# The first pass of a two-layer image kernel: groups of 1, 4, 4, ... tiles, and three of them by Strassen's seven block products

## The chip, the cores and the metric

The kernel runs on one core of one Trainium2 chip. The metric is the device time of the kernel in microseconds (us); three runs of the kernel before have a median of 2600.22 us (2597.3 to 2600.9). The engines are TensorE (PE; its weight loads are PEld), VectorE (DVE), ScalarE (ACT), GpSimd (POOL) and SyncE (SP, which issues most DMAs). Each engine runs its own instructions in the order in which the program lists them.

## The reference, cut to what matters

The input x has 2 images of 56 x 56 pixels with 384 channels, so 6272 tokens, 49 tiles of 128. All is float32. Layer 0 is a neighbourhood attention and then an MLP. Layer 1 is a projection to 768 channels, a 3x3 depthwise convolution with four decaying scans over the image, a projection back, and an MLP.

```python
# layer 0, after the attention
y = layer_norm(x, ln2_g, ln2_b)
x = x + gelu(y @ w1 + b1) @ w2 + b2          # 384 -> 1536 -> 384
# layer 1
h = _layernorm(x, n1_g, n1_b)
p = h @ w_in + b_in                          # 384 -> 768
local = depthwise_conv3x3(p, k_conv)
mixed = 0.25 * (lr + rl + tb + bt) + local   # decaying scans of local, four directions
x = x + (layernorm(mixed) @ w_out + b_out)   # 768 -> 384
h2 = _layernorm(x, n2_g, n2_b)
return x + gelu(h2 @ w1 + b1) @ w2 + b2
```

## The kernel before, in words

The program has three stages: the attention of layer 0 (not touched, ends near 666 us), a first pass over the tokens (`passes`, from L1446), and a second pass (from L1799) whose second half is called the tail here.

**First pass.** It walks over `groups`, tiles in groups of 2, 3, 4, 4, ... (`sizes`, L625). For group g it does
- the first matmul of layer 0's MLP (`hidden`, L1186, by `columns`, L1176): 12 blocks of 128 hidden channels, each 3 matmuls over the 384 channels, with the group's tokens as the moving side (up to 512 wide), then a gelu on ACT,
- `project_in` (L1468) of the group before, which is called `waiting`: 6 blocks with w_in, evicted by ACT and stored to p_d,
- the second matmul (`tokens`, L1194): 12 matmuls of 384 columns for each tile; VectorE adds the residual x and measures the result x2 for the next layer norm.

Each float32 matmul is two instructions in the trace, each with a weight load of its own.

Between the 12 blocks m of the first matmul stand, written out by hand, the steps for two other groups. For the waiting group: `norm_w.shift` at m = 1 (VectorE), the normalization by ACT (`apply_by_scalar`, L239) from m = 2, `turned` (L1160, 16 transposes of 32x32 blocks by VectorE for a tile) from m = 3, `scaled` (L1169, ACT) at the last block, `store_x2` (L1492). For the next group: its statistics at m = 3 (`norm_of`), `shift` at m = 5, the normalization from m = 7, and `add_row` (L1113) at the end. The next group's `turned` and `scaled` follow behind project_in. `Norm.close` (L219) ends a set of statistics with one small VectorE operation and a pow on GpSimd; `shift` on VectorE waits for that pow. Two x tiles and two xn tiles exist at a time (pool x), so the load of group g + 2 (`load_group`, L1578, at the end of group g) can start when the last read of group g's x is over.

While the convolution has nothing to do (groups 1 to 3), tiles are turned by VectorE (`by_vector`, L1507); later the transposes are made by TensorE (`channels`, L1155). The convolution (`Band`, `Columns`, all on VectorE with some ACT and GpSimd) is dealt out by `Beside` (L115): every call of `beside.go(worth)` adds 0.9 x worth of credit and issues the next steps of the convolution while there is credit, each at a cost that the program states; `until` (L168) issues all that is left of a job. The first band's jobs exist when `project_in` has covered the first 20 lines of the image, at the end of `project_in` for group 2, which runs in group 3.

`prepare_w_out` (L1120) runs in group 1: 12 small matmul instructions, a trip through DRAM, and a pass of VectorE over w_out.

PSUM in this pass: two banks for the second matmul (y and y_end), three for transposes (ps_t) and three for the first matmul (ps_m).

**The tail.** Six groups of four tiles of the second pass do both MLP matmuls by Strassen's scheme with seven block products. `hidden_by_seven` (L1637) splits the 512 tokens into halves a and b, the first 256 of the 384 channels into two blocks of 128, and the hidden channels into halves; the third block of channels is done plainly. In each of three rounds u it issues 11 adds of 2 matmuls with 256 columns (22 instead of the plain 24 halves) into the banks ua (one), uz (two) and ub (two, reused in place: ACT copies a bank out between products). `finish(u)` completes a round in the middle of the next one; the last is called from the projection that follows. `measuring` is a generator whose steps are issued twice a round. `tokens_by_seven` (L1719) does the same for the second matmul with 192 columns. The sums that the scheme needs are made by GpSimd: `sums_of_w1` (5 operations) and `sums_of_w2` (4) once, `sums_of_input` (4) for each group, `sums_of_hidden` (3) for each round.

Of the kernel before, what the change touches and what calls it, by code (L numbers as in the profile page):

```python
# [175 lines left out]
def block_kernel(ctx: ExitStack, tc: tile.TileContext, ins: dict, out: bass.AP):  # L176
# [70 lines left out]
    def to_channels(psum, xs, dst, nch, g, b):  # L247

        n = xs[0].shape[0]
        for c in range(nch):  # L250
            tp = psum.tile([P, len(xs) * n], F32, name="tp", tag="pt")
            for k, x in enumerate(xs):
                nc.tensor.transpose(
                    tp[:, k * n : (k + 1) * n], x[:, c * P : (c + 1) * P], ident[:n, :n]
                )
            nc.scalar.activation(  # L256
                dst[:, c, : len(xs) * n], tp, AF.Identity, bias=col(b, c), scale=col(g, c)
            )
# [366 lines left out]
    sizes = [2, 3] + [NT] * ((T2 // P - 5) // NT)  # L625
# [444 lines left out]
    def passes(xs, xn, w1, w2, between=lambda ps: None):  # L1070
# [5 lines left out]
        cctx, bctx = ExitStack(), ExitStack()  # L1076
        cp = cctx.enter_context(tc.tile_pool(name="conv", bufs=2))
        ps_y = bctx.enter_context(tc.tile_pool(name="psy", bufs=1, space=PSUM))
        ps_t = bctx.enter_context(tc.tile_pool(name="pst", bufs=3, space=PSUM))
        ps_m = bctx.enter_context(tc.tile_pool(name="psm", bufs=3, space=PSUM))  # L1080
# [39 lines left out]
        def prepare_w_out():  # L1120
# [16 lines left out]
            t = flat(half("sums", "work"))  # L1137
# [17 lines left out]
        def channels(xn, n, g, b):  # L1155
            hT = io.tile([P, NC, MT], F32, name="hT")
            to_channels(ps_t, [xn[:, k, :] for k in range(n)], hT, NC, g, b)
# [18 lines left out]
        def columns(w, m, hT, n, name="mm"):  # L1176

            ps = ps_m.tile([P, MT], F32, name=name)
# [7 lines left out]
        def hidden(w1, m, hT, n, b1, name="mm"):  # L1186
            ps = columns(w1, m, hT, n, name)
# [258 lines left out]
        x = xs.pop(0)  # L1446
        hT = channels(xn, groups[0][1], "L0_conv_ln2_g", "L0_conv_ln2_b")
# [4 lines left out]
        add_row(x, groups[0][1], "b2_0")  # L1452
# [12 lines left out]
        waiting = None  # L1465
        bands = [(b, lo, hi) for b in range(B) for lo, hi in BANDS[b]]

        def project_in(g, hT, between=lambda: None):  # L1468
            t0, n = groups[g]
            pt = io.tile([P, NI, MT], F32, name="mx")  # L1470
            for m in range(NI):
# [5 lines left out]
                if m == 1:  # L1477
                    between()
# [23 lines left out]
        ln2, n1 = ("L0_conv_ln2_g", "L0_conv_ln2_b"), ("L1_conv_n1_g", "L1_conv_n1_b")  # L1502

        for g, (t0, n) in enumerate(groups):
            hid = []

            by_vector = 0 < g < last and not beside.busy()  # L1507
            preparing = prepare_w_out() if g == 1 else iter(())
            if g == last:
                beside.until((0, NI - 1))  # L1510
                load_row(0, "b2_1")
                ahead = load_mix(0)
            for m in range(NHID):
                next(preparing, None)
                if waiting is not None:
                    gw, x2w, norm_w = waiting
                    if m == 1:
                        norm_w.shift(groups[gw][1])
                    if m == 2:
                        xn_w = xp.tile([P, NT, C], F32, name="xn")  # L1520
                    if 2 <= m < 2 + groups[gw][1]:
                        norm_w.apply_by_scalar(m - 2, x2w, xn_w)
                    if by_vector and m == 2:
                        hT_w = io.tile([P, NC, MT], F32, name="hT")
                    if by_vector and 3 <= m < 3 + groups[gw][1]:
                        turned(xn_w, m - 3, hT_w)
                    if m == (11 if g == 1 else 6):
                        store_x2(gw, x2w)
                    if m == NHID - 1 and by_vector:
                        scaled(hT_w, groups[gw][1], *n1)  # L1530
                    elif m == NHID - 1:
                        hT_w = channels(xn_w, groups[gw][1], *n1)
                hid.append(hidden(w1, m, hT, n, "L0_conv_b1"))
                if g < last:
                    if m == 3:
                        x_next, n_next = xs.pop(g + 1), groups[g + 1][1]
                        norm_next = norm_of(x_next, n_next, sm)
                        norm_next.close(n_next)
                    if m == 5:
                        norm_next.shift(n_next)  # L1540
                    if m == 7:
                        xn_next = xp.tile([P, NT, C], F32, name="xn")
                    if 7 <= m < 7 + n_next:
                        norm_next.apply_by_scalar(m - 7, x_next, xn_next)
                    if m == NHID - 1:
                        add_row(x_next, n_next, "b2_0")
                if g == last:
                    measure_beside(m, 0, ahead)
                beside.go(MLP)
            for _ in preparing:  # L1550
                pass
            if g == 0:
                between(bank())
            if waiting is not None:
                project_in(gw, hT_w)
            if g == last:
                w1, w2_1, w_parts = weights(1)
                for part in w_parts[:3]:
# [412 lines left out]
```

## Time and profile before

| what | value |
|---|---|
| median of three runs | 2600.22 us |
| the profiled execution's own time | 2597.61 us |
| its span | 2595.7 us |
| TensorE busy, mean granted clock | 2575.3 us (99%), 0.999 |
| VectorE / ACT / GpSimd busy | 2004.2 / 959.2 / 406.1 us |
| first transposes and first matmul of the first pass | 666.27 and 667.34 us |
| start of group 1 / 2 / 3 / 4 on TensorE | 699.76 / 759.85 / 833.32 / 910.63 us |
| start of the tail's first round | 2157.18 us |

Times in a row of the timeline are the start in us from the start of the span, the length in us, then engine, line, operation, names (out<-in), shape and count; in brackets stand the idle time ahead of it and what ended it. The line of a helper stands for all its callers. TensorE's matmuls overlap at their ends, so that the pace of a row is read from start to start. "Busy" on GpSimd is rough.

### The profile page before, as it was taken

How to read it: one execution, taken by the hardware profiler on the slowest of the kernel's cores; microseconds unless marked ns; L12 is line 12 of the kernel's file. 1: busy time of each engine (PE TensorE's matmuls, PEld its weight loads, DVE VectorE, ACT ScalarE, POOL GpSimd, SP SyncE). 2: the span in 40 equal slices, each digit the busy share in tenths (PEclk: the TensorE clock that was granted, in tenths of full speed). 3: DMA queues.
4: the chain of work that ended last, by engine and by line, in shares of the span. 5: the costliest groups of instructions: out<-in, count | busy, mean ns of one | idle time of the engine just before them, and what ended most of it. 6: DMA issues, size and time to landing. Idle time of an engine off the chain costs nothing. (4 is left out here: it accounts for less than half of the span.)

```text
span 2595.7 us, 39312 instructions
## 1 busy us (share of the span) xinstructions
PE 2575.3 (99%) x15781; PEld 1593.0 (61%) x15782; DVE 2004.2 (77%) x3669; ACT 959.2 (37%) x1679; POOL 406.1 (16%) x404
## 2 busy tenths in 40 slices
PE   9999999999999999999999999999999999999999
PEld 5666666666555544555545555555555557888888
DVE  3888978887364687788998789889988836888871
ACT  4655655655332232322344422312233312333222
POOL 0111211111110100000010000000010042344342
PEclk9999999999999999999999999999999999999999
DMA  7422454225311132332346534433354321111000
GB/s 224 149 93 95 159 185 148 82 96 199 110 37 40 55 126 84 116 108 100 127 163 236 190 129 165 174 124 122 113 210 167 140 100 43 50 49 49 22 13 18
DMA packets 131649, 299.12 MB, mean 115 GB/s; under 512 B 10390, under 2 KB 86528, under 8 KB 129152
## 3 DMA queue, kind: packets, MB, share of 16 engines
q1 hardware_dynamic: 126512, 269.76, 30.1%
q10 hardware_dynamic: 4944, 26.74, 3.0%
q8 instruction: 126, 2.06, 0.3%
q14 instruction: 67, 0.55, 0.1%
HBM read 180.86 MB, written 115.61 MB: 114 GB/s over the span
## 5 line engine op out<-in xcount | busy, mean ns | idle before, releaser
L1180 PE MATMUL mm<-hT,w 128*128 128x512 f32 (+2 forms) x1368 | 575.0, 576 | 0.4 <-ACT hT L256 0.2
L1180 PEld LDWEIGHTS mm<-hT,w 128*128 128x128 f32 x1368 | 256.4, 190 | 286.3 <-issue 266.6
L1276 DVE SCALAR_TENSOR_TENSOR loc<-pt,taps,loc 128x990 f32<-128x990 f32 (+9 forms) x336 | 377.0, 1122 | 10.0 <-ACT loc L1258 1.7
L1191 ACT ACTIVATE hid<-mm,chan 128x512 f32<-128x512 f32 (+2 forms) x228 | 152.3, 668 | 502.0 <-PE mm L1180 502.0
L224 POOL TENSOR_TENSOR rs<-rs,mhalf 128x4 f32<-128x4 f32 (+4 forms) x72 | 89.2, 1239 | 1360.9 <-DVE rs L221 1359.9
L1198 PE MATMUL y_end<-w,hid 128*128 128x384 f32 x912 | 300.4, 486 | 0.0
L1198 PE MATMUL y<-w,hid 128*128 128x384 f32 x864 | 284.5, 486 | 0.0
L545 DVE TENSOR_TENSOR pts<-sc,bias 119x448 f32<-119x448 f32 (+5 forms) x396 | 219.0, 615 | 45.9 <-PE sc L534 45.5
L555 ACT ACTIVATE pts<-pts 119x448 f32<-119x448 f32 (+5 forms) x396 | 210.7, 573 | 107.1 <-DVE pts L545 102.5
L1198 PEld LDWEIGHTS y_end<-w,hid 128*128 128x128 f32 x912 | 172.8, 190 | 118.7
L1198 PEld LDWEIGHTS y<-w,hid 128*128 128x128 f32 x864 | 163.5, 190 | 112.5 <-issue 1.0
L1164 DVE STREAM_TRANSPOSE hT<-xn 32x96 f32<-32x96 f32 x672 | 181.2, 270 | 36.9 <-ACT xn L242 16.4
L388 PE MATMUL ps<-hT,wqkv 128*128 128x448 f32 x504 | 206.6, 554 | 2.1 <-ACT vs L433 1.5
L1180 PE MATMUL mm<-hT,w_in 128*128 128x512 f32 (+2 forms) x468 | 191.9, 569 | 0.6 <-ACT hT L256 0.6
L1180 PEld LDWEIGHTS mm<-hT,w_in 128*128 128x128 f32 x468 | 88.5, 190 | 102.0 <-issue 90.3
L388 PEld LDWEIGHTS ps<-hT,wqkv 128*128 128x128 f32 x504 | 92.0, 191 | 85.3 <-issue 75.3
L242 ACT ACTIVATE xn<-xc,sh,rs 128x384 f32<-128x384 f32 x98 | 64.7, 698 | 169.9 <-DVE sh L235 169.7
L1409 DVE STREAM_TRANSPOSE turned<-mx 32x192 f32<-32x192 f32 x336 | 123.9, 369 | 4.4
L534 PEld LDWEIGHTS sc<-qT,kT 32*100 32x100 f32 (+3 forms) x3168 | 87.8, 169 | 46.6 <-DVE sum L564 7.6
L574 PE MATMUL o<-pts,vt 100*32 100x112 f32 (+3 forms) x3168 | 115.2, 262 | 0.4 <-ACT pts L555 0.4
L534 PE MATMUL sc<-qT,kT 32*100 32x112 f32 (+3 forms) x3168 | 106.5, 269 | 3.4 <-DVE pts L545 3.4
L604 PE MATMUL ps<-wproj,og 128*128 128x384 f32 x294 | 104.8, 496 | 2.8 <-DVE og L517 2.2
(168 smaller groups left out, 3656.6 us busy)
## 6 DMA issues: line engine op xcount, KB each, us to landing
loc<-loc_d SPq DMA_DIRECT2D x24, 784.0 KB
mixed<-mix_d SPq DMA_DIRECT2D x24, 784.0 KB
mix_d<-mixed SPq DMA_DIRECT2D x24, 784.0 KB
xa<-x_d SPq DMA_DIRECT2D x23, 768.0 KB
bias<-in_bias_t ACTq DMA_DIRECT2D x13, 1344.0 KB
mx<-mix_d SPq DMA_DIRECT2D x11, 1536.0 KB
p_d<-mx SPq DMA_DIRECT2D x10, 1536.0 KB
pt<-p_d SPq DMA_DIRECT2D x18, 560.0 KB
```

Of the source, the lines that this page charges most:

```text
L388: nc.tensor.matmul(ps, lhsT=wqkv[:, c, m * P : (m + 1) * P], rhs=hT[:, c, half_of(n)], start=c == 0, stop=c == NC - 1,)
L534: nc.tensor.matmul(sc[i // 2][: w.keys, i % 2, q : q + TT], lhsT=kT[d, hg, w.keys_at + r * w.kc : w.keys_at + (r + w.rows) * w.kc], rhs=qT ...
L545: nc.vector.tensor_tensor(self.pts[:n, h : h + 2, lo:hi, :], sc[half][:n, :, at * TT : (at + hi - lo) * TT].rearrange("p h (c q) -> p h c ...
L555: nc.scalar.activation(t, t, AF.Exp)
L574: nc.tensor.matmul(o[i * HD : (i + 1) * HD, self.slot, :TT], lhsT=w.vt[:n, c, h * HD : (h + 1) * HD], rhs=self.pts[:n, i, c, :], start=c = ...
L604: nc.tensor.matmul(ps, lhsT=ogs[t // 7][:, c, at : at + P], rhs=wproj[:, c, :], start=c == 0, stop=c == NC - 1,)
L1164: nc.vector.transpose(hT[j : j + HD, :, k * P + i : k * P + i + HD], xn[i : i + HD, k, :].rearrange("p (c q) -> p c q", c=NC)[:, :, j : j ...
L1180: nc.tensor.matmul(ps[:, : n * P], lhsT=w[:, c, m * P : (m + 1) * P], rhs=hT[:, c, : n * P], start=c == 0, stop=c == NC - 1,)
L1191: nc.scalar.activation(t[:, : n * P], ps[:, : n * P], AF.Gelu, bias=col(b1, m))
L1198: nc.tensor.matmul(ps, lhsT=t[:, k * P : (k + 1) * P], rhs=w[:, m, :], start=m == 0, stop=m == len(lhs) - 1,)
L1276: nc.vector.scalar_tensor_tensor(to, pt[:, lo + dy - self.top : hi + dy - self.top, xt : xt + n], self.tap(dy, dx), to, ALU.mult, ALU.add,)
L1409: nc.vector.transpose(t[j : j + HD].rearrange("p (m c) -> p m c", m=NI)[:, :, i : i + HD], mx[i : i + HD, :, k * P + j : k * P + j + HD],)
```

## The change

The groups become 1, 4, 4, ...: one tile, then twelve groups of four. Groups 1 to 3 (`EARLY`) do both MLP matmuls with the functions of the tail, which take the bias, the source and the destination as arguments now and give back control between products. Their buffers (sums of the weights, of the input and of the hidden values) come from a pool named first, which lies where the convolution's buffers come later: it is closed at group 4, and only then are the convolution's pool and the former PSUM pools opened. Up to then the PSUM banks are those of the tail; project_in, the plain first matmul of group 0 and the first transposes use the two uz banks. `open_banks` opens these banks and clears three of them with zero matmuls. `prepare_w_out` moves from group 1 to group 4 and takes its buffer from another tag. In groups 0 to 3 the next group's statistics move from m = 3 to m = 0 and 1; in groups 1 to 3 the waiting group's tiles are turned at every other m, the next group's between the products of the second matmul, and `finish` of the last round comes behind the first column of project_in.

```diff
-    sizes = [2, 3] + [NT] * ((T2 // P - 5) // NT)
+    sizes = [1] + [NT] * (T2 // P // NT)
+    EARLY = range(1, 4)
...
-        cp = cctx.enter_context(tc.tile_pool(name="conv", bufs=2))
-        ps_y = bctx.enter_context(tc.tile_pool(name="psy", bufs=1, space=PSUM))
-        ps_t = bctx.enter_context(tc.tile_pool(name="pst", bufs=3, space=PSUM))
-        ps_m = bctx.enter_context(tc.tile_pool(name="psm", bufs=3, space=PSUM))
+        tp = fctx.enter_context(tc.tile_pool(name="first", bufs=1, reuse_waits="tile"))
...
-            t = flat(half("sums", "work"))
+            t = flat(half("sums", "out", 3))
...
-        x = xs.pop(0)
-        hT = channels(xn, groups[0][1], "L0_conv_ln2_g", "L0_conv_ln2_b")
         load_row(0, "b2_0")
...
-        def project_in(g, hT, between=lambda: None):
+        def project_in(g, hT, between=lambda: None, at=1):
...
+        def open_banks(stack, name):
+            ps_y = stack.enter_context(tc.tile_pool(name=f"psy_{name}", bufs=1, space=PSUM))
+            ps_d = stack.enter_context(tc.tile_pool(name=f"psd_{name}", bufs=1, space=PSUM))
+            ps_u = stack.enter_context(tc.tile_pool(name=f"psu_{name}", bufs=2, space=PSUM))
+            bank_b = ps_d.tile([P, 2, C // 2], F32, name="yb")
+            banks_b = [ps_d.tile([P, 2, MT // 2], F32, name=f"ub{i}") for i in range(2)]
+            zeros = tp.tile([P, MT], mybir.dt.bfloat16, name="zeros")
+            nc.vector.memset(zeros, 0.0)
+            for t in (bank_b, *banks_b):
+                t = flat(t)
+                nc.tensor.matmul(
+                    t, lhsT=zeros[:, :P], rhs=zeros[:, : t.shape[1]], start=True, stop=True
+                )
+            return ps_y, ps_u, bank_b, banks_b
+
+        ps_y, ps_u, bank_b, banks_b = open_banks(fctx, "first")
+        ps_t = ps_m = ps_u
+        tag = "uz"
+        w1_sums = sums_of_w1(w1, tp.tile([P, NC, HID // 2], F32, name="w1_t"))
+        x = xs.pop(0)
+        hT = channels(xn, groups[0][1], "L0_conv_ln2_g", "L0_conv_ln2_b")
+        add_row(x, groups[0][1], "b2_0")
+
+        for g, (t0, n) in enumerate(groups):
+            if g == EARLY.stop:
+                fctx.close()
+                cp = cctx.enter_context(tc.tile_pool(name="conv", bufs=2, reuse_waits="tile"))
+                ps_y = bctx.enter_context(tc.tile_pool(name="psy", bufs=1, space=PSUM))
+                ps_t = bctx.enter_context(tc.tile_pool(name="pst", bufs=3, space=PSUM))
+                ps_m = bctx.enter_context(tc.tile_pool(name="psm", bufs=3, space=PSUM))
+                tag = "pt"
+            early = g in EARLY
+            by_vector = early or 0 < g < last and not beside.busy()
+            preparing = prepare_w_out() if g == EARLY.stop else iter(())
...
+            def ahead_of(m):
...
+                    if m == 1:
+                        norm_w.shift(nw)
+                    if m == 2:
+                        xn_w = xp.tile([P, NT, C], F32, name="xn")
+                    if 2 <= m < 2 + nw:
+                        norm_w.apply_by_scalar(m - 2, x2w, xn_w)
...
+                    k = (m - 3) // 2 if early else m - 3
+                    if by_vector and 0 <= k < nw and (m % 2 == 1 or not early):
+                        turned(xn_w, k, hT_w)
+                    if m == 6:
+                        store_x2(gw, x2w)
+                    if m == NHID - 1 and by_vector:
+                        scaled(hT_w, nw, *n1)
...
+            def behind(m):
...
+                    if g < EARLY.stop and 2 * m < n_next:
+                        for k in range(2 * m, min(2 * m + 2, n_next)):
+                            norm_next.add(k, [x_next[:, k, :]])
...
+                    if m == (1 if g < EARLY.stop else 3):
+                        norm_next.close(n_next)
+                    if m == 5:
+                        norm_next.shift(n_next)
...
+                    if 7 <= m < 7 + n_next:
+                        norm_next.apply_by_scalar(m - 7, x_next, xn_next)
+                    if m == NHID - 1:
+                        add_row(x_next, n_next, "b2_0")
+
+            def both():
+                for m in range(NHID):
+                    ahead_of(m)
+                    behind(m)
+                    if m % 2 == 1:
+                        yield
+
+            if early:
+                s1, s2 = (tp.tile([P, NHID // 2, MT // 2], F32, name=x) for x in ("s1", "s2"))
+                low, high, finish = hidden_by_seven(
+                    hT, xsums, w1, w1_sums, (s1, s2), both(), "L0_conv_b1"
+                )
+                project_in(waiting[0], hT_w, finish, 0)
...
+            if early:
+                for i, _ in enumerate(tokens_by_seven(low, high, s1, s2, w2, w2_sums, x, x2)):
+                    if 0 <= i < n_next:
+                        turned(xn_next, i, hT)
+                    if i == 5:
+                        scaled(hT, n_next, *ln2)
+                        xsums = sums_of_input(hT) if g + 1 in EARLY else None
+                    if i == 6:
+                        for k in range(2, n):
+                            norm.add(k, [x2[:, k, :]])
+                for k in range(2):
+                    norm.add(k, [x2[:, k, :]])
...
+            if g == 0:
+                hT = channels(xn_next, n_next, *ln2)
+                xsums, w2_sums = sums_of_input(hT), sums_of_w2(w2)
+            norm.close(n)
+            waiting = g, x2, norm
+            if g + 2 <= last:
+                xs[g + 2] = load_group(x1f, groups[g + 2], "xa")
```

In the early groups `beside.go` is called from project_in alone, not behind the blocks of the first matmul or the tiles of the second. The second pass keeps its order.

## The prediction

> **What bounds the kernel now.** I read the page first, then the TensorE timeline of the first pass, then the same timeline where the kernel already works by seven products, and last the queues of VectorE, GpSimd and SyncE around these two places.
>
> The page's rows by engine and by slice:
>
> ```profile
> PE 2575.3 (99%) x15781; PEld 1593.0 (61%) x15782; DVE 2004.2 (77%) x3669; ACT 959.2 (37%) x1679; POOL 406.1 (16%) x404
> ...
> PEclk9999999999999999999999999999999999999999
> ```
>
> TensorE is busy in 2575.3 of 2595.7 us and its clock is never cut. So every matmul taken out shortens the kernel, and every wait put in on TensorE lengthens it one for one. TensorE's timeline of one first-pass group of four tiles (start, us, engine, line, operation, count):
>
> ```profile
> 833.32 31.06 PE L1180 MATMUL mm<-hT,w 128*128 128x512 f32 x72
> 864.22 15.61 PE L1180 MATMUL mm<-hT,w_in 128*128 128x512 f32 x36
> 879.67 7.90 PE L1198 MATMUL y<-w,hid 128*128 128x384 f32 x24
> ...
> 910.63 28.49 PE L1180 MATMUL mm<-hT,w 128*128 128x512 f32 x66
> ```
>
> No row has a wait. From the starts: first matmul 30.90 us (72 at 0.429), project_in 15.45, second matmul 910.63 - 879.67 = 30.96 (96 at 0.3225), 77.3 in all. The same timeline in the tail, where six groups are done by seven:
>
> ```profile
> 2300.50 1.03 PE L1653 MATMUL ua<-hT,w 128*128 128x256 f32 x4
> 2301.84 1.13 PE L1653 MATMUL uz<-xsums,w_t 128*128 128x256 f32 x4 [0.32 <-POOL xsums L1634]
> 2302.81 1.03 PE L1653 MATMUL ub<-xsums,w_t 128*128 128x256 f32 x4
> 2303.68 1.89 PE L1653 MATMUL ua<-hT,w 128*128 128x256 f32 x8
> ...
> 2345.06 4.06 PE L1740 MATMUL y<-w,hid 128*128 128x192 f32 x24
> ...
> 2372.36 1.03 PE L1653 MATMUL ua<-hT,w 128*128 128x256 f32 x4
> ```
>
> 2303.68 to 2305.40 is 8 matmuls, so 0.2158 each, and 2345.06 to 2372.36 is 168, so 0.1625 each. A half-width matmul costs half: the saving of seven products for eight is real on this chip, and the tail waits only 0.32 us per group. What the tail does not have is the first pass's VectorE work:
>
> ```profile
> 705.98 4.51 DVE L1164 STREAM_TRANSPOSE hT<-xn 32x96 f32<-32x96 f32 x16 [3.47 <-ACT xn L242]
> 710.52 0.56 DVE L216 BATCH_NORM_STATS2 st<-xa 128x6 f32<-128x384 f32 x1
> ...
> 713.40 4.51 DVE L1164 STREAM_TRANSPOSE hT<-xn 32x96 f32<-32x96 f32 x16
> ```
>
> Turning one tile (turned) holds VectorE for 4.52 us in one piece; the tail's steps between products are 3.03 (eight L1409 transposes). The statistics of four tiles take 713.40 - 710.52, about 0.7 a tile. GpSimd, where the sums of the weights are made in the tail:
>
> ```profile
> 2094.28 1.81 POOL L1621 TENSOR_TENSOR w_t<-w 128x768 f32<-128x768 f32 x1
> ...
> 2103.24 2.60 POOL L1709 TENSOR_TENSOR w_t<-w 128x1152 f32<-128x1152 f32 x1
> ...
> 2113.65 1.02 POOL L224 TENSOR_TENSOR rs<-rs,mhalf 128x4 f32<-128x4 f32 x1
> ```
>
> The pow of a layer norm (L224) stands behind these sums in GpSimd's queue. And SyncE's row of a group's load, with the traffic from 699 to 711 us in slices of 0.3 us:
>
> ```profile
> 700.59 0.37 SPq L631 DMA_DIRECT2D xa<-x_d  x1
> ```
> ```profile
> GB/s 0 0 0 0 0 0 0 0 41 113 82 138 384 394 404 404 384 266 10 0 0 0 0 0 0 0 0 0 0 0 0 0 55 0 0 0 0 0 0 0
> ```
>
> It is issued when the last read of the old buffer ends (700.52) and lands near 704.7: 4.1 us.
>
> **What is saved.** Three groups: first matmul 132 x 0.2158 = 28.49 for 30.90, second 168 x 0.1625 = 27.30 for 30.96; 6.07 a group, **-18.2** in all. The weight loads do not take this back: the tail has the same loads in these paces.
>
> **Regrouping.** The first five tiles as 1 + 4 instead of 2 + 3. 128-column matmuls run at 0.116 (72 L1180 on uz in 8.35 us, 2575.7 to 2584.1). Before 72 x (0.2158 + 0.3225) + 36 x (the same) = 58.1; after 72 x (0.116 + 0.429) + 36 x (the same) = 58.9: **+0.8**.
>
> **Start.** The first transposes now stand behind three zero matmuls, these behind a memset that VectorE has after the decay memsets (667.9 + 0.27), where they waited for bad (666.2). Hidden starts at 670.3 instead of 667.3: **+3.0**. The one-tile group has two banks instead of three, and ACT's four normalizations (0.7) fall between its gelus, while the transposes of the next four tiles now come behind the tokens instead of ahead of them, so their evictions show: 0.3 + 0.3 + 0.3 + 0.6 + 0.2 = **+1.7**. The five sums of w1 (9.0 us) on GpSimd I let begin at 661, when its last attention work ends (pow at 660.2 + 0.7): by the sizes in the code their buffers lie over the closed key pool. They are then over before the row of b2 lands (672.2 in this trace) and cost nothing; if they had to wait for the last residual (to 670), hidden by that cover no longer, +4.5.
>
> **Waits inside the three groups.** I put each engine's instructions of one group in program order with durations from the rows, T the start of its first product: adds on VectorE 0.66 (L1672, L1699), copies on ACT 0.57, gelu pairs 0.84 to 0.91, normalizations 0.6 behind one another, 0.07 from one engine to the next, all from the timelines of the tail and of this pass. This walk applied to the tail gives 72.1 us a group, where the trace has 71.86 (2300.50 to 2372.36), so it is about 0.5 a group too dark. Groups 2 and 3:
>
> - x_next is now measured at the first step, not at m = 3. Its load goes out when the last add of the group before (result(0,1)) has freed the buffer, T+1.4, and lands at T+5.7. VectorE stands still until then, and the shift of the waiting group is queued behind two of the statistics: T+7.3. ACT then normalizes two tiles (2 x 0.6) ahead of its copy of u2, done T+9.3. TensorE, free at T+7.8 (nine steps of 4 x 0.2158), needs the copy: **1.5**.
> - VectorE has two more statistics, turned(0) to T+13.5, then u2's add to T+14.1. Until that has read bank uz, TensorE may not add to it: **3.2**.
> - turned(1) stands ahead of u1's add, that ahead of a gelu on ACT, that ahead of the next copy of u1: **2.6**; the same once more **0.9**.
> - scaled(hT_w), queued on ACT ahead of the last copy, waits for turned(3), and project_in waits for it: **1.9**. Its second column reuses the bank that u1's last add still reads: **1.0**.
>
> In sum 11.1 a group, 22.1 for two. In group 1 the load is early enough, but norm.close is called behind sums_of_w2: its pow comes 4 x 2.62 us later, about T+13.4, the shift waits, ACT's apply and the copy of u2 behind it, and TensorE stands from T+7.9: **7.7**; u2's add behind two statistics and turned(0): 3.8; scaled and the bank 1.4 + 1.0. **13.9.** All other work hides beside TensorE (VectorE has 8 x 4.52 of turned and about 13 of adds and statistics in the 71 us of a group; GpSimd has 29.5 in a tail group): it is order, not load, that hurts.
>
> **Convolution.** Its first band starts one token stage later, 4 x 6.2 x 0.9 = 22 us of the planner's credit. Stepping the planner's costs through both versions, nothing is forced in front of the last group, and 5.9 instead of 3.0 us ahead of the load for the half-way group, whose transposes at 2088.4 stand close behind a load issued at 2085.8: 0 to 3, I take **+1.5**. prepare_w_out moves from group 1 to group 4, same matmuls: 0; its VectorE pass (4.8 us) meets convolution there, hidden by two y banks of 7.7 us each.
>
> **Sum.** -18.2 + 0.8 + 3.0 + 1.7 + 13.9 + 22.1 - 1.5 (the walk's excess) + 1.5 = **+23.3** on the profiled execution's own 2597.6 us (span 2595.7). That execution lies 2.6 under the median of the runs; I round to **2621**. Bounds of the waits from the same walk: with loads that land at once and the pow ahead of the w2 sums the three groups wait 22.4 us, not 36: 2607. Loads 2 us later (+3.8), the late w1 sums (+4.5) and 3 us at half-way (+1.5): 2631.
>
> [...]
>
> **Rivals.**
> - **Queues keep pace as in the tail, so faster.** For it: 0.3 us a group there, and VectorE is busier (60 of 72 us). Against: steps of 4.5 instead of 3.0, late loads, the pow. Without the group waits -18.2 + 0.8 + 3.0 + 1.7 = -12.7: 2585. It decides if all waits in the three groups stay under 12.7 us.
> - **Only the w2 sums bite** (GpSimd's queue in group 1, 13.9), groups 2 and 3 run freely: 2599, no change.
> - **More than the walk**: w1's sums late, the clock cut: 2632 to 2640, slower still.
>
> **Chances.** Forecast 0.70, faster rival 0.14, no change 0.08, more 0.08. The range 2604 to 2636 covers the bounds and most of the worse case and leaves out the faster one. A measurement of this kernel tells about 0.2% from no change: faster 0.14, same 0.08, slower 0.78.
>
> **What would show it.** TensorE's timeline: L1653-type rows at 0.216 and tokens at 0.1625 (else the saving is wrong); one wait near 7.7 us on a ub bank in group 1, released by ACT; waits of 1.5 and 3.2 in groups 2 and 3, the latter by VectorE's u2 add; GpSimd's pow right behind four 2.6 us sums. Groups 2 and 3 near 82 us. If they last 72, the prediction is wrong at the waits.

## The result, and the profile after

The changed kernel takes 2638.48 us (median of four runs, 2632.01 to 2640.87), the kernel before 2600.56 beside it (four runs, 2597.3 to 2605.4): the ratio is 1.014, 95% interval 1.0115 to 1.0165. That is 37.9 us slower. Forecast were +20 to +23 (2621, range 2604 to 2636): the direction held, the size did not.

The profiled execution of the changed kernel took 2640.24 us, its span 2638.4. 28 executions of the kernel before, timed beside e5 to e8, spread from 2594.5 to 2606.6 us, with a granted clock of 1.000 in the lowest four and 0.997 in the highest four, and the profiled one (0.999) lies low among them. In the changed kernel's profile the attention's last projection begins at 660.61 us for 657.52 and takes 9.70 us for 8.01: 4.8 us of the two spans' difference arise there, ahead of the first pass. For the most part they are the clock, which is 0.50 from 634 to 640 us and 0.61 from 660 to 664 here and 1.00 in both stretches before. By experiment e8 they are not the change's.

The page's rows of the changed kernel, by engine and by slice:

```profile
PE 2578.7 (98%) x16181; PEld 1655.7 (63%) x16181; DVE 2020.2 (77%) x3691; ACT 984.2 (37%) x1751; POOL 479.7 (18%) x473
...
PEclk9999999999899999999999999999999999999999
```

The span grew by 42.7 us (4.8 of them in the attention), the busy time by 3.4, although 17.4 us of matmul work (-18.2 + 0.8) should have gone. So some 39 us are new waits of TensorE, and some 21 us are matmuls that took longer than forecast, most of them at half the clock: the mean granted clock is 0.991 for 0.999, and TensorE is busy for 35.5 us at a clock of 0.50, for 3.4 in the kernel before. The row of the clock shows it in one slice alone (its share of 2638.4 us is 660 to 726 us, the first pass's beginning). From the end of that projection to the start of group 4 both kernels do the same work, but for prepare_w_out's matmuls (4.4 us, which move behind it): 670.31 to 934.96 us is 264.6, 665.53 to 910.63 was 245.1, so that the first pass is 24.0 us slower there, and the rest of the kernel 13.9. TensorE's timeline of group 2, by seven products:

```profile
771.59 1.03 PE L1545 MATMUL ua<-hT,w 128*128 128x256 f32 x4
...
780.77 1.13 PE L1545 MATMUL ub<-hT,w_t 128*128 128x256 f32 x4 [1.12 <-ACT hid_u L1590]
...
785.75 1.10 PE L1545 MATMUL uz<-xsums,w 128*128 128x256 f32 x4 [2.98 <-DVE hid_u L1591]
...
793.25 1.35 PE L1545 MATMUL ub<-xsums,w_t 128*128 128x256 f32 x4 [2.95 <-ACT hid_u L1583]
...
825.93 4.06 PE L1632 MATMUL y<-w,hid 128*128 128x192 f32 x24
...
853.23 1.03 PE L1545 MATMUL ua<-hT,w 128*128 128x256 f32 x4
```

From 825.93 to 853.23 is 168 matmuls in 27.30 us, 0.1625 each: the saving is there as forecast. But group 2 lasts 853.23 - 771.59 = 81.64 us, where its matmuls alone need 28.49 + 15.45 + 27.30 = 71.24; group 3 lasts 81.73 with much the same waits. Group 1, from 695.11 to 771.59, lasts 76.48 where its matmuls need 60.0:

```profile
710.61 2.07 PE L1545 MATMUL ub<-hT,w_t 128*128 128x256 f32 x4 [7.33 <-ACT hid_u L1590]
712.47 1.91 PE L1545 MATMUL ub<-hT,w_other 128*128 128x256 f32 x4
716.18 2.05 PE L1545 MATMUL uz<-xsums,w 128*128 128x256 f32 x4 [1.79 <-DVE sh L235]
718.02 1.91 PE L1545 MATMUL uz<-hT,w 128*128 128x256 f32 x4
719.73 1.92 PE L1545 MATMUL ub<-xsums,w_t 128*128 128x256 f32 x4
721.43 2.35 PE L1545 MATMUL ua<-hT,w 128*128 128x256 f32 x8
723.62 1.03 PE L1545 MATMUL ub<-xsums,w_t 128*128 128x256 f32 x4
```

Read the second column: four matmuls of 256 columns take 1.03 us in group 2 and 1.9 to 2.07 behind the 7.33 us wait. From 710.61 to 723.62 stand 28 matmuls: 13.01 us, less the 1.79 us wait 11.22, where 28 x 0.2158 = 6.04 would do. The granted clock is 0.50 from 706 to 722 us, and the 28 matmuls take 5.2 us more. GpSimd's timeline shows what the 7.33 us waited for, the norm's pow behind four sums of w2:

```profile
698.18 2.62 POOL L1601 TENSOR_TENSOR w_t<-w 128x1152 f32<-128x1152 f32 x1
700.88 2.61 POOL L1601 TENSOR_TENSOR w_t<-w,w_t 128x1152 f32<-128x1152 f32 x1
...
708.59 0.56 POOL L224 TENSOR_TENSOR rs<-rs,mhalf 128x1 f32<-128x1 f32 x1
```

So far the forecast. What it did not have stands behind group 4, where no code of the MLPs changed (TensorE's timeline again):

```profile
1376.15 15.72 PE L1179 MATMUL mm<-hT,w_in 128*128 128x512 f32 x36 [2.97 <-ACT hT L256]
...
1597.31 0.85 PE L1396 MATMUL xi<-ident,mx 128*128 128x128 f32 x6 [2.63 <-DMA mx<-mix_d]
...
1965.71 0.55 PE L1396 MATMUL xi<-ident,mx 128*128 128x128 f32 x3 [2.76 <-DVE st L216]
...
2131.02 0.30 PE L1396 MATMUL xi<-ident,mx 128*128 128x128 f32 x1 [2.96 <-DMA mx<-mix_d]
```

Four waits, 11.3 us, none of which the kernel before has. The row of the first place in the kernel before:

```profile
1342.51 15.61 PE L1180 MATMUL mm<-hT,w_in 128*128 128x512 f32 x36
```

How the convolution comes into it, ACT's timeline says for the first wait:

```profile
1369.46 0.97 ACT L1322 COPY line<-loc 128x392 f32<-128x392 f32 x1 [1.43 <-DMA loc<-loc_d]
1371.69 2.56 ACT L1322 COPY line<-loc 128x392 f32<-128x392 f32 x3 [1.26 <-DMA loc<-loc_d]
1374.14 0.69 ACT L1190 ACTIVATE hid<-mm,chan 128x512 f32<-128x512 f32 x1
1374.72 0.71 ACT L242 ACTIVATE xn<-xa,sh,rs 128x384 f32<-128x384 f32 x1
1375.32 2.11 ACT L256 ACTIVATE hT<-tp,chan 128x512 f32<-128x512 f32 x3
```

ACT has the convolution's four copies in its queue ahead of the eviction (L256) that TensorE needs. The copies wait for a load of loc_d that had not landed. ACT is busy 37% of the span; it is late all the same, because its queue is in order. For the second, SyncE issues the load of mix_d at 1587.76 us, 3.5 us after its group began (1584.22); in the kernel before it went out 1.9 us ahead of the group. For the third, VectorE's statistics (L216), which free the bank, stand behind a scan of the convolution:

```profile
1963.41 1.79 DVE L1226 TENSOR_TENSOR_SCAN line<-decay,line 128x784 f32<-128x784 f32 x1
1965.12 1.00 DVE L216 BATCH_NORM_STATS2 st<-xi 128x6 f32<-128x384 f32 x2
```

The fourth is the half-way group that the prediction had named.

### The profile page after: what moved, and what is told of

The parts are those of the page before. It is cut to its first block, busy times and chain, and to the rows that moved or that the text cites. A ratio compares the mean times of both kernels' runs of the same rounds, so it can differ in the third digit from the quotient of the medians.

```text
span 2638.4 us, 40304 instructions
## 1 busy us (share of the span) xinstructions
PE 2578.7 (98%) x16181; PEld 1655.7 (63%) x16181; DVE 2020.2 (77%) x3691; ACT 984.2 (37%) x1751; POOL 479.7 (18%) x473
## 5 line engine op out<-in xcount | busy, mean ns | idle before, releaser
L1179 PE MATMUL mm<-hT,w 128*128 128x512 f32 x1080 | 475.3, 595 | 0.1
L1179 PEld LDWEIGHTS mm<-hT,w 128*128 128x128 f32 x1080 | 202.4, 191 | 239.9 <-issue 233.6
L1190 ACT ACTIVATE hid<-mm,chan 128x512 f32<-128x512 f32 x180 | 123.3, 685 | 401.2 <-PE mm L1179 401.1
L1197 PE MATMUL y<-w,hid 128*128 128x384 f32 x744 | 245.1, 486 | 0.0
L1197 PE MATMUL y_end<-w,hid 128*128 128x384 f32 x744 | 245.0, 486 | 0.0
L1197 PEld LDWEIGHTS y_end<-w,hid 128*128 128x128 f32 x744 | 140.8, 190 | 96.7
L1197 PEld LDWEIGHTS y<-w,hid 128*128 128x128 f32 x744 | 140.7, 190 | 96.4 <-issue 0.5
L1179 PE MATMUL mm<-hT,w_in 128*128 128x512 f32 x360 | 156.4, 593 | 3.1 <-ACT hT L256 3.0
L1179 PEld LDWEIGHTS mm<-hT,w_in 128*128 128x128 f32 x360 | 68.1, 190 | 89.6 <-issue 80.8
L604 PE MATMUL ps<-wproj,og 128*128 128x384 f32 x294 | 107.3, 505 | 2.8 <-DVE og L517 2.2
```

The costliest lines, as they stand in the source:

```text
L604: nc.tensor.matmul(ps, lhsT=ogs[t // 7][:, c, at : at + P], rhs=wproj[:, c, :], start=c == 0, stop=c == NC - 1,)
L1179: nc.tensor.matmul(ps[:, : n * P], lhsT=w[:, c, m * P : (m + 1) * P], rhs=hT[:, c, : n * P], start=c == 0, stop=c == NC - 1,)
L1190: nc.scalar.activation(t[:, : n * P], ps[:, : n * P], AF.Gelu, bias=col(b1, m))
L1197: nc.tensor.matmul(ps, lhsT=t[:, k * P : (k + 1) * P], rhs=w[:, m, :], start=m == 0, stop=m == len(lhs) - 1,)
```

## The experiments

**Theory:** the saving is as forecast, the waits of groups 1 to 3 are order in the queues as the walk had them, and what is missing is the convolution's later start, which shifts its copies, loads and stores against the groups of matmuls. **Rivals:** all of it is load, so that a wait taken away comes back elsewhere; or the late waits come from prepare_w_out or the pools, not from the convolution's start. The times of the kernel before beside each set differ by little: e1 to e4 had it at 2601.33 (seven runs), e5 to e8 at 2600.79 (28), e9 and e10 at 2601.48 (16), e11 and e12 at 2600.30 (15).

### e1: the norm closed ahead of the sums of w2

```diff
-                xsums, w2_sums = sums_of_input(hT), sums_of_w2(w2)
+                xsums = sums_of_input(hT)
             norm.close(n)
+            if g == 0:
+                w2_sums = sums_of_w2(w2)
```

> The changed kernel, with group 0's norm.close ahead of sums_of_w2 in GpSimd's queue. Theory (the pow behind the sums is what holds group 1): the wait of 7.3 us on ub in group 1 goes, the matmul rows at half pace after it too, group 1 lasts 64 to 67 us instead of 76.5, groups 2 and 3 stay at 81.7; total 10 us under the changed kernel. Rival (VectorE's turned is what holds group 1): it stays above 72 us.

Measured: 2631.82 us (2629.22 to 2635.88), ratio 1.0123, interval 1.0104 to 1.0143, 6.7 under the changed kernel where 10 were expected. The 7.33 us wait is gone and most of the half clock behind it (mean clock 0.995 for 0.991). Group 1 lasts 692.75 to 761.03 = 68.28 us, 8.2 less; a wait of 4.35 us on VectorE's add (L1591) stays. The pow's place in GpSimd's queue is the cause of the long wait. That the group missed the 64 to 67 has a second cause, found in e6 and shown in e9 and e10.

### e2: the convolution's planner catches up

```diff
             hid = []
+            if EARLY.stop <= g < EARLY.stop + 3:
+                beside.rate = 1.0 if g < EARLY.stop + 2 else 0.9
```

> The changed kernel, with the planner's rate at 1.0 instead of 0.9 in groups 4 and 5, so that the convolution is back where it stood in the kernel before by group 6. Theory (the four waits of about 3 us behind group 4, 11.3 us in all, come from the convolution's later start): most of them go, total 7 to 11 us under the changed kernel. Rival (they come from the convolution's pool, which is opened later over other buffers, or from prepare_w_out in group 4): all four stay, same time.

Measured: 2635.62 (2633.25 to 2637.32), ratio 1.0132, interval 1.0115 to 1.0150: only 2.9 under the changed kernel, not 7 to 11. Three of the four late waits go (1376, 1965, 2131), the one of 1597 grows to 6.67 us. TensorE's row and SyncE's rows of that place:

```profile
1600.00 1.51 PE L1396 MATMUL xi<-ident,mx 128*128 128x128 f32 x6 [6.67 <-DMA mx<-mix_d]
```
```profile
1589.51 0.32 SPq L1282 DMA_DIRECT2D loc_d<-loc  x1
1590.36 0.70 SPq L1373 DMA_DIRECT2D mx<-mix_d  x1
```

The load of mix_d, whose data were stored long before (1533.56), stands in SyncE's queue behind a store of the convolution that waits for VectorE, and is issued at 1590.36, 7.5 us after TensorE began the group at 1582.87. In the kernel before it went out at 1549.04, 1.9 us ahead of its group. So how much is done matters less than what stands in the queue when a group begins.

### e3: the kernel before, with the convolution started late

```diff
-                if g < last or k < n - 1:
+                if (g < last or k < n - 1) and g != 3:
                     beside.go(ROW)
```

> The kernel before, with the planner's credit for the four tiles of group 3 left out: only the convolution's start is later, by 22 us of credit, as in the changed kernel. Theory: waits of about 3 us each on TensorE appear behind group 4, 8 to 12 us in all, the time is 2609 to 2612. Rival (pool or prepare_w_out): 2600 to 2603, no new wait but at most one ahead of the half-way group (0 to 3 us, as the prediction had it).

Measured: 2615.23 (2611.42 to 2616.46), ratio 1.0058, interval 1.0041 to 1.0074: 13.9 us slower, by four calls left out of the kernel before. TensorE's timeline shows the same four waits at the same lines:

```profile
1343.51 17.41 PE L1180 MATMUL mm<-hT,w_in 128*128 128x512 f32 x36 [2.00 <-ACT hT L256]
...
1566.54 1.51 PE L1397 MATMUL xi<-ident,mx 128*128 128x128 f32 x6 [2.82 <-DMA mx<-mix_d]
...
1936.26 0.55 PE L1397 MATMUL xi<-ident,mx 128*128 128x128 f32 x3 [2.40 <-DVE st L216]
...
2101.85 0.30 PE L1397 MATMUL xi<-ident,mx 128*128 128x128 f32 x1 [3.25 <-DMA mx<-mix_d]
```

The waits sum to 10.5, within the 8 to 12 expected. The time is 3 us above the expectation: the rows behind two of them take longer (36 matmuls in 17.41 us here, 15.61 in the kernel before; 6 in 1.51, 0.82 before). The rival of prepare_w_out and the pools falls, since neither is changed here.

### e4: the waiting tiles turned by TensorE in groups 1 to 3

```diff
-                    if by_vector and 0 <= k < nw and (m % 2 == 1 or not early):
-                        turned(xn_w, k, hT_w)
+                    if early:
+                        for k in {5: (0, 1), 7: (2,), 9: (3,)}.get(m, ()):
+                            if k < nw:
+                                turned_by_tensor(xn_w, k, hT_w, *n1)
```

turned_by_tensor is three transposes by TensorE into one bank and three evictions by ACT with the norm's gain and bias, in place of turned and scaled.

> The changed kernel, with the waiting group's tiles in groups 1 to 3 turned by TensorE into the y banks (3 transposes a tile) and brought to hT by ACT with scale and bias, instead of turned and scaled. Theory (VectorE's pieces of 4.5 us ahead of its short adds make the waits in groups 2 and 3): these groups last 74 to 76 us instead of 81.7, the waits on u2's add and on the copy of u1 go; total 14 to 18 us under the changed kernel. Rival (the late load of x_next makes them): 79 us or more.

Measured: 2621.24 (2619.82 to 2623.58), ratio 1.0077, interval 1.0061 to 1.0094: 17.2 under the changed kernel. Groups 2 and 3 last 73.74 and 73.72 us, 8 less, with no wait of 0.4 us or more. The starts of groups 2 and 3 on TensorE:

```profile
765.73 1.03 PE L1557 MATMUL ua<-hT,w 128*128 128x256 f32 x4
...
839.47 1.03 PE L1557 MATMUL ua<-hT,w 128*128 128x256 f32 x4
```

The waits of these groups were VectorE's 4.5 us pieces ahead of its adds, as walked, and did not come back elsewhere. This run takes the pieces off VectorE altogether, so that by itself it doesn't tell their order from their load. Group 1 keeps its wait for the pow (6.88 us), and the four late waits stay (1.99 to 3.30).

### e5: four repairs of order together

e1, e2 and e4, and in groups 1 to 3 the next group's statistics back at m = 3:

```diff
-                    if g < EARLY.stop and 2 * m < n_next:
+                    if g == 0 and 2 * m < n_next:
...
-                    if g >= EARLY.stop and m == 3:
+                    if g > 0 and m == 3:
```

> The changed kernel with four repairs of order: norm.close ahead of sums_of_w2, the waiting tiles turned by TensorE in groups 1 to 3, the next group's statistics back at m = 3 in these groups, and the planner's rate at 1.0 in groups 4 and 5. Theory (the loss is order in the queues, and each wait goes with its own cause): group 1 falls from 76.5 to about 62 us, groups 2 and 3 from 81.7 to 73.7 each (as the run that turned by TensorE alone had it), 31 us in all, and three of the four late waits go, less the longer one near 1600 us, about 4.6 us: 2638 - 36 = 2603 us. If the repairs merely add up as measured alone (-6.7, -17.2, -2.9): 2611. Rival (the waits have one common cause, such as VectorE's load, and taking one away lets the next one grow): 2615 or more, with waits above 3 us in groups 1 to 3.

Measured: 2607.89 (2606.62 to 2611.13), ratio 1.0031, interval 1.0016 to 1.0046: 30.6 under the changed kernel, between the two sums that were written down for the theory, and far from the rival's. Groups 2 and 3 last 72.68 and 73.47 us. Left are 2.05 and 1.54 us in group 1, 2.79 at the start and 6.55 near 1568, on the load of mix_d.

### e6: the same, with early zeros and the load issued by ACT

```diff
-            zeros = tp.tile([P, MT], mybir.dt.bfloat16, name="zeros")
-            nc.vector.memset(zeros, 0.0)
...
+    zeros = const.tile([P, 512], mybir.dt.bfloat16, name="zeros")
+    nc.vector.memset(zeros, 0.0)
...
-                    nc.sync.dma_start(
+                    (nc.scalar if g == 0 else nc.sync).dma_start(
                         out=mx[:, lo:hi, here : here + size],
```

> The run with all four repairs, and two more: the zeros for the zero matmuls are written at the start of the kernel, and the second pass's first load of mix_d is issued by ACT instead of SyncE, where it stood behind stores that wait for VectorE. Theory: the wait of 2.8 us at the start of the first pass goes (-2.5 to -3), and the wait near 1600 us (6.7 us with the planner's rate at 1.0) falls under 1: together 8 to 9 us under the run with four repairs, about 2595, below the kernel before (2600.5). Rival (the load is late because the convolution's results are late, not because of SyncE's queue): the wait near 1600 stays at 5 us or more, and the time is 3 under the run with four repairs. If ACT is held up by the load, gelus are late instead and TensorE waits for ACT near 1585.

Measured: 2596.39 (2594.02 to 2602.64), ratio 0.9989, interval 0.9978 to 0.9999, 11.5 under e5, where 8 to 9 were expected. ACT issues the load at 1519.68, some 30 us ahead of the group; the transposes that need it run without a wait, and the start waits 0.65 us for VectorE instead of 2.79. What was left in group 1 is read from VectorE's and GpSimd's timelines:

```profile
695.90 2.57 DVE L237 SCALAR_TENSOR_TENSOR sh<-mv,rs 128x1 f32<-128x1 f32 x1 [3.86 <-POOL rs L226]
...
701.17 2.58 DVE L223 SCALAR_TENSOR_TENSOR rs<-mv,ones 128x4 f32<-128x4 f32 x1
703.68 0.68 DVE L1605 TENSOR_TENSOR hid_u<-uz,hid_u 128x512 f32<-128x512 f32 x1
```
```profile
695.84 2.62 POOL L1615 TENSOR_TENSOR w_t<-w 128x1152 f32<-128x1152 f32 x1
...
701.12 2.62 POOL L1615 TENSOR_TENSOR w_t<-w 128x1152 f32<-128x1152 f32 x1
```

Operations of 1 and 4 numbers a partition last 2.57 and 2.58 us; elsewhere they take 0.16 (675.62 in e9, for one). Both end with GpSimd's sum (695.84 + 2.62 = 698.46; 701.12 + 2.62 = 703.74). The add that TensorE waits for stands behind the second.

### e7: groups 1 and 2 only

```diff
-    EARLY = range(1, 4)
+    EARLY = range(1, 3)
```

with the other repairs of order and early zeros, and no change of the planner's rate.

> Only groups 1 and 2 by seven block products, with norm.close ahead of sums_of_w2, TensorE turning the waiting tiles, the statistics at m = 3 and early zeros; the convolution's buffers are opened at group 3, so its first band starts in group 3 as in the kernel before. No change of the planner's rate. Theory (the four late waits of about 3 us come from the convolution's start in group 4): none of them, and the time is 2600.5 - 12.1 (two groups saved) + 0.8 + 1.7 (regrouping and group 0) + 2 + 2.5 (what is left in groups 1 and 2) + 3.5 (the attention's end) = 2599. Rival (the late waits come from something else in the early groups): they stay, 2610.

Measured: 2601.13 (2599.43 to 2606.08), ratio 1.0008, interval 0.9997 to 1.0018. The convolution begins in group 3 as before, and of the four late waits nothing over 0.75 us is left. The theory holds; two groups' saving (12.1) is just used up by what the change adds.

### e8: the regrouping alone, in the kernel before

```diff
-    sizes = [2, 3] + [NT] * ((T2 // P - 5) // NT)
+    sizes = [1] + [NT] * (T2 // P // NT)
```

> The kernel before with groups of 1, 4, 4, ... tiles and nothing else. The attention before it issues the same instructions in the same order up to the loads of x. Theory: +0.8 of narrower matmuls and up to 1.7 of shorter cover in group 0, 2601 to 2603, convolution on time, no late waits. If the attention's end is 3 to 4 us later here too, as in all profiles of the changed kernel so far, the loads of x by 1 + 4 tiles are what does it: 2605. If it is not, that comes from something else in the program.

Measured: 2602.74 (2598.52 to 2604.21), ratio 1.0008, interval 0.9999 to 1.0017: +1.95. TensorE's rows at the end of the attention:

```profile
660.56 9.70 PE L604 MATMUL ps<-wproj,og 128*128 128x384 f32 x24 [2.15 <-DVE og L517]
...
671.00 0.52 PE L253 MATMUL tp<-ident,xn 128*128 128x128 f32 x3 [0.74 <-DVE bad L924]
```

The first transposes come at 671.0, not 666.3, in this profile, with the last projection taking 9.70 us for 8.01, as in the changed kernel's profile, where the clock beside it is 0.61. But the median rose by 2 only, and this kernel's executions spread over the same clocks (1.000 to 0.997). And e11, with 1 + 4 tiles too, begins that projection at 656.87. So a late end of the attention is taken here for a matter of the execution's clock (mean 0.997 in e8's profile, 0.999 before; six matmuls of L604 take 3.82 us from 637.95 in e8's, 2.20 from 636.22 before), not for a cost of the loads by 1 + 4 tiles, as the expectation had offered. That is argued from medians: none of the profiles is of the kernel before at a mean clock of 0.997.

### e9 and e10: the sums of w2 in group 0

```diff
                         norm_next.close(n_next)
+                        if g == 0:
+                            w2_sums = sums_of_w2(w2)
```

in place of the call at the end of group 0; e9 is e6 with it, e10 the changed kernel with it alone.

> The run with repaired orders and loads (2596), and GpSimd's sums of w2 moved from the start of group 1 into group 0, behind the next group's pow. In that run VectorE's smallest operations, of 4 numbers a partition, lasted 2.57 and 2.58 us instead of 0.16 in group 1, each to the end of the 2.62 us sum that GpSimd was at, and TensorE waited 2.04 and 1.55 us behind them. Theory (GpSimd's operation holds up VectorE's operation with two inputs): both waits go, group 1 falls from 65.7 to about 62, 3.6 us in all: 2593. Rival (the small operations were long for a reason of their own, such as the pow they wait for): they stay at 2 us or more in group 1 and the time stays at 2596. If the sums hold up group 0 instead, a wait of 2 us or more shows there.

> The changed kernel with that one move: the sums of w2 made in group 0. The pow of group 0's norm then stands behind nothing in group 1, and no sum runs beside VectorE's small operations. Theory: the wait of 7.3 us goes; group 1 falls from 76.5 to 66 to 67, 1.2 to 2 under the run that only closed the norm ahead of the sums (68.3), because the two small operations that lasted 1.63 and 1.33 there take 0.16; time 2638 - 9 or 10 = 2629. Rival (only the pow's place counts): 68.3, 2632, as in that run. The other waits, of groups 2 and 3 and behind group 4, stay.

Measured: e9 2595.30 (2592.22 to 2597.49), ratio 0.9976, interval 0.9966 to 0.9985; e10 2626.41 (2621.42 to 2634.40), ratio 1.0098, interval 1.0081 to 1.0116. Group 1 falls to 61.60 us in e9 and to 64.04 in e10 (e1: 68.28), its waits in e9 are gone, and the small operations last 0.16 there. The cost has in part moved to group 0. VectorE's and GpSimd's timelines of e9:

```profile
679.03 2.58 DVE L237 SCALAR_TENSOR_TENSOR sh<-mv,rs 128x4 f32<-128x4 f32 x1 [3.25 <-POOL rs L226]
...
697.96 0.16 DVE L237 SCALAR_TENSOR_TENSOR sh<-mv,rs 128x1 f32<-128x1 f32 x1 [3.86 <-POOL rs L226]
```
```profile
678.97 2.62 POOL L1615 TENSOR_TENSOR w_t<-w 128x1152 f32<-128x1152 f32 x1
```

That shift now lasts 2.58 us beside the first sum, ACT's normalizations wait for it, and TensorE waits 1.66 us in group 0. So against the kernel before, measured beside each, the gain went from 4.4 us (e6) to 6.2, not by the 3.6 of group 1's waits; the two intervals overlap, so that the times alone don't show these 1.8 us, the rows of group 1 do. e10's group 1 came 2 us lower than expected. e9 is the best of the versions: 6.2 us under the kernel before, 43 under the changed one.

### e11: the sums one step later

```diff
                     if m == 5:
                         norm_next.shift(n_next)
+                        if g == 0:
+                            w2_sums = sums_of_w2(w2)
```

> The run with w2's sums in group 0 (2595), with these sums one step later: behind the next group's shift instead of ahead of it. There the shift, an operation of 4 numbers a partition, lasted 2.58 us beside GpSimd's first sum, ACT's normalizations waited for it, and TensorE waited 1.66 us in group 0. Theory: the shift takes 0.17 again, the wait falls under 0.6, time 2593.5 to 2594.5. Rival (the wait comes from the order of ACT's normalizations alone): it stays at 1.7 and the time at 2595.

Measured: 2596.45 (2591.89 to 2601.03), ratio 0.9987, interval 0.9976 to 0.9999: no better than e9, and within its interval. The expectation was wrong in a simple way: the shift lasts 2.58 us again, and the wait is 1.53. VectorE's row and GpSimd's:

```profile
675.02 2.58 DVE L237 SCALAR_TENSOR_TENSOR sh<-mv,rs 128x4 f32<-128x4 f32 x1 [3.04 <-POOL rs L226]
```
```profile
674.96 2.62 POOL L1615 TENSOR_TENSOR w_t<-w 128x1152 f32<-128x1152 f32 x1
```

The shift waits for the pow; GpSimd's next instruction, the sum, waits for nothing once the pow is over and starts 0.06 us ahead of the shift. The later line in the program did not put it behind VectorE's instruction.

### e12: the changed kernel with the late waits taken away

Only the rate (as in e2) and the load by ACT (as in e6).

> The changed kernel with only the planner's rate at 1.0 in groups 4 and 5 and the first load of mix_d issued by ACT; groups 1 to 3 and the start as changed. Theory (the step that failed is the convolution's later start, which costs four waits of 2.6 to 3.0 us, 11.3 in all, with some matmuls at half the clock behind them): all four go, 2638.5 - 11.3 - 1 = 2626, about as much under the changed kernel as the kernel before rose when its convolution alone was started late (14). Rival (rate and load only move the waits): 2633 or more, with a wait above 3 us behind group 4.

Measured: 2623.52 (2622.11 to 2624.88), ratio 1.0083, interval 1.0069 to 1.0097: 15.0 under the changed kernel. Of the four late waits the places of the first two read now:

```profile
1369.94 15.61 PE L1179 MATMUL mm<-hT,w_in 128*128 128x512 f32 x36
...
1588.69 0.82 PE L1396 MATMUL xi<-ident,mx 128*128 128x128 f32 x6
```

Two waits of 0.59 and 0.79 us at other places (1450.63 and 1610.73) are all of 0.4 us or more that is left behind group 4, up to the tail's zero matmuls. Not all of the 15.0 is theirs: in this profile group 4 begins at 931.88 us for 934.96, since groups 1 to 3 came 3.9 us shorter without being changed. So about 12 of the 15.3 us between the two spans are the late waits and the clock behind them.

## Why the prediction missed

**The step that failed** is "Convolution. [...] nothing is forced in front of the last group, and 5.9 instead of 3.0 us ahead of the load for the half-way group [...]: 0 to 3, I take +1.5". It measured 13.9 us when put into the kernel before by itself (e3) and about 12 when taken out of the changed kernel (e12, of 15.0 in all). Of the four places the step had only the half-way group in view, and there it held: that wait is 2.96 us. The other three it put at nothing. The step asked whether the convolution would be finished in time, by the planner's costs, and it was, but for the half-way load. It did not ask what stands in the queues of ACT, SyncE and VectorE when each group of matmuls begins. The copies of the convolution on ACT, its stores on SyncE and its scans on VectorE lie in the queues between instructions that TensorE needs. The kernel before has an alignment of these in which TensorE waits 0.58 and 0.99 us at the most behind group 4; a shift of 22 us of the planner's credit loses it at four places. For the other engines' instructions I had walked the queues of groups 1 to 3 only, not those behind.

**The other terms:**

| term of the sum | forecast | measured |
|---|---|---|
| saving of three groups | -18.2 | paces 0.2158 and 0.1625 as forecast |
| regrouping and group 0 | +2.5 | +1.95 (e8, with the old banks; not clear of zero) |
| wait at the start | +3.0 | 2.86 us wait on the zeros |
| group 1 (73.4 us with the walk's excess taken off) | +13.4 | 76.48 us, +16.5 |
| groups 2 and 3 (81.8 each) | +21.1 | 81.64 and 81.73 us, +20.9 |
| convolution's later start | +1.5 | +12 (e12) to +13.9 (e3) |

By the right-hand column the sum is -18.2 + 1.95 + 2.86 + 16.5 + 20.9 + 12 to 13.9 = 36 to 37.9; measured were 37.9. Without the last term it is 24.0, as the two profiles have it ahead of group 4. The walk of each engine's queue gave groups 2 and 3 to 0.2 us in sum, and the 7.7 us wait of group 1 to 0.4. In groups 2 and 3 the sum is in part luck, for the walk was not right wait by wait: the first three of group 2 came as 1.12, 2.98 and 2.95 for 1.5, 3.2 and 2.6, the later ones smaller, and the waits of 0.4 us and more sum to 7.5 of the 10.4 us; the rest is smaller waits and matmuls at half the clock (1.8 us from 793.25 to 797.63), of which the walk had none.

Group 1 was 3.1 us too low because of the clock, for which the sum has no term: the prediction reads it as "never cut" in the trace of before. That was a misreading. TensorE's rows of the attention's beginning, before:

```profile
9.64 7.03 PE L388 MATMUL ps<-hT,wqkv 128*128 128x448 f32 x18 [0.62 <-ACT hT L364]
...
26.92 8.73 PE L388 MATMUL ps<-hT,wqkv 128*128 128x448 f32 x18 [1.48 <-ACT vs L433]
```

The same 18 matmuls take 1.7 us more, and the granted clock is 0.50 from 28 to 30 us; in slices of 65 us, and as a mean of 0.999, it could not be seen. The trace of after shows more of it: 28 matmuls at half their pace behind a wait of 7.33 us, 5.2 us. Part of it covered the waits that the walk had behind (3.8 became 1.79). The half clock lasted to 722.35 us here, 11.7 us from the end of that wait, across a second wait.

**Of the rivals,** "queues keep pace as in the tail" fell: the waits of 0.4 us and more in the three groups sum to 24.3 us, not to less than 12.7. After seven repairs (e9) it comes near: groups 2 and 3 at 72.7 us. "Only the w2 sums bite" fell at groups 2 and 3. "More than the walk" named w1's sums, which were in time (663.79 to 672.8), and the clock, which took 5.2 us; the time lies in its 2632 to 2640, but mostly for another reason. Why the clock falls at the attention's end in some executions and not in others, which e8's expectation put down to the loads, is open.

## What to carry to other kernels

Where work is dealt out beside a bound engine, a change that shifts its start must be walked through the queues of every engine up to the end, not only priced by its amount: here the shift cost 12 to 14 us, most of the 18.2 that was saved. A saving on the bound engine is kept only if every instruction ahead of its next input, on every in-order queue, is walked too: with seven repairs the change's 18.2 us became a gain of 6.2 (0.24%). A load whose data are long ready should not stand in a queue behind a store that waits (6.67 us of TensorE's time in e2).

## What the runs showed of the hardware

VectorE's small operations on two inputs lasted to the end of a GpSimd sum on two inputs that had begun 0.05 to 0.06 us ahead of them: 1 or 4 numbers a partition took 2.57 and 2.58 us beside a 2.62 us sum, ending within 0.02 us of it, and 0.16 or 0.17 without it (e6, e9, e11). I had priced GpSimd's sums at nothing but their own queue. The statistics, with one input, kept their 0.53 us beside the same sums (699.07 in e6). Why the small operations lasted as long as the sum, no run here shows.

TensorE's half clock came behind a wait of 7.33 us, but also behind waits of 1.48 us and less (the attention before, at 28 us), and the same wait was followed by a slow row or not: at one place four matmuls took 2.04 us behind 2.98 us of wait in e12 (785.15), and 1.10 behind 2.98 in the changed kernel (785.75), where the clock stayed at 1.00. In the changed kernel the half clock came behind 2.95 us (793.25: twelve matmuls in 4.38 us).

In the record of the granted clock of the changed kernel's trace, the stretches of 0.50 ahead of the trace's end are six of 3.41 us, one of 6.83 and one of 17.07. The longest, 705.28 to 722.35 us, begins within the 7.33 us wait; the one behind the 2.95 us wait is 794.03 to 797.44. What sets the clock, no run here tests.

Nor did a slow row always cost time. In e12 four matmuls took 2.04 us behind the 2.98 us wait (785.15), and the next wait shrank from 2.95 to 1.46: the row behind it came 7.51 us later, in the changed kernel 7.50. So a wait of 2 to 3 us near TensorE had a price here that differed by up to 1.8 us from one place or execution to the next.
